# A graph network on one core: the first convolution's bias on the features instead of on attention's output, with the order around it changed

## The chip, the core and the metric

One core of a Trainium2 chip runs the whole program. The core has TensorE (PE) for matrix products, VectorE (DVE), ScalarE (ACT) and GpSimd (POOL) for elementwise work, and SyncE (SP), which issues most of the transfers. The metric is the device time of one execution in microseconds (us), as the median of several runs.

## The reference

128 graphs of 128 nodes, 512 features per node, float32 throughout. Two layers follow each other, each with a residual and a layer norm.

```
feats = x @ W                              # 8 heads of 64
e     = leaky_relu(feats@a_self [:,None] + feats@a_neigh [None,:], 0.2)
att   = softmax(e + -1e10 * (1 - adj))
x     = layernorm(x + relu(att @ feats + b))
...
H     = (adj != 0);  Dn = 1/(H @ adj[0]);  Be = 1/H.sum(0)
conv(x, W, b) = Dn * (H @ (Be * (H.T @ (x @ W.T)))) + b
h     = layernorm(relu(conv(x, W1, b1)), gamma, beta)     # 1024 features
x     = layernorm(2 * x + conv(h, W2, b2))
```

Each row of att sums to one. So att @ (feats + b) equals att @ feats + b.

## The kernel before, in words

Two graphs, g = 0 and 1, form a pair, and 64 pairs p are worked through as a software pipeline. A pair runs through four stages, each one period after the last: stage 0 prepares the adjacency matrix, stage 1 makes the features and scores, stage 2 the softmax and attention with the first norm, stages 3 and 4 the second layer. In a steady period the engines therefore work on several pairs at once.

No scheduler decides the order. Each step is a function that is registered with a stage and a time within a nominal period of 38.6: `at(2, 28.05, add_bias, ...)` is stage 2 at 28.05. At the end all steps of all pairs are sorted by (p + stage) * 38.6 + time and emitted in that order (L1223). These numbers are only keys for sorting. [...] A table `first` (L1159) and two small ones in the last loop override the keys of the first and last pairs.

Each of the three large products of a pair (features `pf`, hidden layer `ph`, second weights `py`) is done by seven half-size products instead of eight (function `chain`, L325). The products go in the order 1, 2, 6, 5, 7, 4, 3 and use three accumulators X, Y, W. Product 1 starts X; 6, 7 and 4 add to it. After 1, 6 and 7 ACT copies X away (`copy`, L343), since DVE needs those intermediate states; product 6 must wait for the first copy, 7 for the second, 4 for the third. The sums that go in are made on POOL: `x_sums` (xS, L468), `z_sums` (zS, L837) and `h_sums` (hS, L468).

Steps that matter below, by engine, with the names that the profile shows:

- DVE: `attended_pair` (L733, L734) divides attention's output by its row sums, giving y. `residual` (L748) is relu and adding of x, `moments` (L756, L757) the mean and variance. `sum_blocks` (L947 to L952) reduces the sums of squares of the hidden layer, which go through memory (`write_sums` L957, `read_sums` L963) and come back in `sum_rest` (so, L971). `y_sum` (L932) puts the second product together, `x_transpose` (L384) turns x for the next features, `edges` (L420 to L427) and `scale_edges` (hB, L434) and `nodes` (L359 to L368) prepare the adjacency matrix, `r_evict` (R, L450) makes the propagator. `largest` (nm, L610) takes row maxima. `h_sum` (L863) puts the hidden layer together. `y_scale` (L1004) normalizes, `skip` (L802) starts the output o, `o_sum` (L1021) adds to it, `e_transpose` (eT, L639) turns the exponentials.
- POOL: `add_bias` (L739) adds b to y; `rstds` (rsa and rso, L764) is the power -0.5 of a variance; `mask` (neg, L377) makes the mask and `masked` (L588) adds it to the scores nb, in four parts (g, q), q being the half of the heads; `h_means` (m, L992) and `h_rstd` (veh L997, rsh L1000) give the hidden layer's norm; `squares` (sq, L901) are folded sums.
- ACT: `leaky` (L604) and `exponential` (L618) on nb, four instructions for each part; `first_output` (L791) writes the first layer's result; `z_evict` (L826) copies the product pz out; `relu` (L878) and `square` (L889) work on the hidden layer h.
- PE: in the order of a period pz, pd, then ph with pq in it, pf with one py in it, attention pav, and the rest of py (all but attention at L97).
- SP: besides others, the row sums rd out and broadcast back as nb (L551, L569), the exponentials out (ed, L622) and back (eb, L630), sd and sums_out, and the loads of x, xb, a, w, ab.

In a steady period before the change, add_bias stands on POOL after the squares and ahead of h_means, mask, rsa and the four masked adds; on DVE sum_blocks, x_transpose 1 and residual 0 follow attended_pair, then y_sum(0,0), residual 1, the variance and y_sum(1,1). h_sum(1,1) comes after skip, hB and nodes. On ACT leaky(0,1) stands after the two z_evict.

The features `ft` hold, for each graph and head, 67 numbers: the two scores, the 64 features and a column of ones that gives attention's row sums. There are two such buffers, used by even and odd pairs.

Of the kernel before, what the change touches and what calls it, by code (L numbers as in the profile page):

```python
# [10 lines left out]
ALU = mybir.AluOpType  # L11
# [9 lines left out]
def kernel(  # L21
# [45 lines left out]
    nc = tc.nc  # L67
# [3 lines left out]
    H = 8  # L71
# [17 lines left out]
    def bank(name):  # L89
        return psum.tile([P, HALF], F32, tag="bank", name=name)  # L90
# [57 lines left out]
    UW = U + 2  # L148
# [16 lines left out]
    def everywhere(t, ap, queue):  # L165
# [5 lines left out]
    b0_bc, b2_bc, bw_bc = (  # L171
        const.tile([P, F], F32, name=n) for n in ("b0_bc", "b2_bc", "bw_bc")
    )
# [37 lines left out]
    for i in range(2):  # L211
        t = const.tile([P, 2, H, UW + 1], F32, name=f"ft{i}")
# [99 lines left out]
    LAST = PAIRS - 1  # L312
    steps = []

    def step(lag, time, since=0, until=PAIRS):

        def keep(fn):
            steps.append((lag, time, fn.__name__, range(since, until), fn, ()))
            return fn
        return keep  # L320

    def at(lag, time, fn, *args, since=0, until=PAIRS):
        steps.append((lag, time, fn.__name__, range(since, until), fn, args))

    def chain(kind, lag, times, multiply, w, extra=0, since=0, until=PAIRS):  # L325

        tag = "chain" if w == HALF else "half"

        def product(p, s, i):
            where, start = {1: ("X", 1), 2: ("Y", 1), 6: ("X", 0), 5: ("W", 1), 7: ("X", 0),
                            4: ("X", 0), 3: ("W", 0)}[i]
            if start:
                s[kind, where] = bank(f"{kind}{where}_{p}")
            multiply(s, i, s[kind, where], start)

        def copy(p, s, i):  # L340
            n = w + (extra if i < 2 else 0)
            t = s[kind, i] = work.tile([P, HALF if w == HALF else FW], F32, tag=f"{tag}_{i}", name=f"{kind}{i}_{p}")
            nc.scalar.copy(t[:, :n], s[kind, "X"][:, :n])  # L343

        for i, t in zip((1, 2, 6, 5, 7, 4, 3), times):
            at(lag, t, product, i, since=since, until=until)
        for i, t in enumerate(times[7:]):
            at(lag, t, copy, i, since=since, until=until)
# [22 lines left out]
    def write_nodes(p, s):  # L371
        s["dd"] = dram.tile([NB, B, B], F32, tag="dd", name=f"dd_d_{p}")
        nc.sync.dma_start(s["dd"].rearrange("b c n -> (b c) n"), s["dr"])
    @step(0, 30.63)
    def mask(p, s):
        s["neg"] = work.tile([P, 2, N], F32, tag="neg", name=f"neg_{p}", bufs=2)
        nc.gpsimd.tensor_scalar(s["neg"], s["a"], -1.0, BIG, op0=ALU.add, op1=ALU.mult)  # L377
# [9 lines left out]
        )  # L387

    at(0, 26.15, x_transpose, 0, since=2)
    at(0, 28.95, x_transpose, 1, since=2)  # L390

    def x_transpose_first(p, s):
        s["px"] = [bank(f"px_{p}_{g}") for g in range(2)]
# [98 lines left out]
    def feature(s, i, to, start):  # L492
# [4 lines left out]
          feature, FW, since=2)  # L497
# [155 lines left out]
        )  # L653

    for (g, q), tm, (lag, tl), (lagx, tx), te, tt in (
        ((0, 0), 31.0, (1, 33.2), (1, 36.1), 4.05, 16.6), ((0, 1), 32.2, (1, 40.63), (1, 40.68), 4.6, 16.65),
        ((1, 0), 34.2, (2, 2.05), (2, 2.1), 7.8, 21.5), ((1, 1), 35.4, (2, 6.0), (2, 7.3), 7.9, 21.55),
    ):
        at(1, tm, masked, g, q)
        at(lag, tl, leaky, g, q)  # L660
        at(lagx, tx, largest, g, q)
        at(2, te, exponential, g, q)
        at(2, tt, e_transpose, g, q, since=1)
# [72 lines left out]
            )  # L736

    def add_bias(p, s, g):
        nc.gpsimd.tensor_tensor(s["y"][:, g, :], s["y"][:, g, :], b0_bc, op=ALU.add)  # L739

    for g, t in enumerate((24.1, 29.2)):
        at(2, t, add_bias, g, until=1)
        at(2, 28.05 + 0.05 * g, add_bias, g, since=1, until=LAST)
        at(2, t, add_bias, g, since=LAST)

    def residual(p, s, g):
        y = s["y"][:, g, :]
# [22 lines left out]
        )  # L770

    at(2, 26.2, residual, 0, until=1)
    at(2, 29.0, residual, 0, since=1, until=LAST)
    at(2, 26.2, residual, 0, since=LAST)
    at(2, 30.7, residual, 1)
    at(2, 30.8, rstds, "a")

    @step(2, 33.12)
    def first_shift(p, s):
# [62 lines left out]
    def hidden(s, i, to, start):  # L842
# [4 lines left out]
        for m in range(KH // 2):  # L847
# [3 lines left out]
                    bool(start) and m == 0 and k == 0, k == KF // 2 - 1,  # L851
                )

    chain("ph", 3, (2.0, 3.8, 5.6, 7.35, 9.1, 12.65, 14.4, 4.0, 5.95, 11.0), hidden,
          HALF)

    def hid(s, g, q):
# [7 lines left out]
        )  # L865

    at(3, 5.9, h_sum, 0, 0, 0, "Y")
    at(3, 11.8, h_sum, 1, 1, 2, "W")
    at(3, 16.4, h_sum, 1, 0, 1, "W")

    def relu(p, s, g, q):
# [45 lines left out]
    def weigh(s, i, to, start):  # L917
# [3 lines left out]
          QU, 1, until=LAST)  # L921
# [62 lines left out]
            s["ve"], s["pm"][:, :2 * N].rearrange("p (g f) -> p g f", g=2), AX.X, ALU.add  # L984
        )

    @step(3, 30.62, until=LAST)
    def h_means(p, s):

        s["m2"] = small.tile([P, 2], F32, tag="m2", name=f"m2_{p}")  # L990
        for g, m in enumerate((s["y2"][:, 0, 0, QU:], s["py", 1][:, QU:QU + 1])):
            nc.gpsimd.tensor_tensor(s["m2"][:, g:g + 1], m, m, op=ALU.mult)  # L992
# [127 lines left out]
    for t, fn, *args in (  # L1120
# [40 lines left out]
        ("nodes", 0): 12.9, ("write_nodes", 0): 12.92, ("spread_nodes", 0): 15.9,  # L1161
        ("edges", 0): 14.46, ("edges", 2): 119.2,
        ("x_transpose", 2, 0): 120.5, ("x_transpose", 2, 1): 121.1, ("scale_edges", 0): 14.47, ("propagator", 0): 14.55,
        ("r_evict", 0): 99.76,
        ("spread_rows", 1): 15.72, ("nodes", 1): 15.55, ("write_nodes", 1): 15.85,
        ("edges", 1): 110.4, ("scale_edges", 1): 110.5, ("neighbours", 1): 80.1,
        ("propagator", 1): 117.76, ("spread_nodes", 1): 80.3, ("r_evict", 1): 121.8,
        ("leaky", 0, 1, 1): 77.65, ("leaky", 0, 0, 1): 73.6, ("largest", 0, 0, 1): 75.3,
        ("attend", 0, 0, 0): 78.95, ("attend", 0, 0, 1): 78.96, ("attend", 0, 1, 0): 78.97,
        ("attend", 0, 1, 1): 78.98, ("attended", 0, 0): 97.8, ("attended", 0, 1): 97.81,  # L1170
        ("add_bias", 0, 0): 97.82, ("add_bias", 0, 1): 97.83,
        ("residual", 0, 0): 99.6, ("residual", 0, 1): 99.65, ("rstds", 0, "a"): 99.7,
        ("leaky", 1, 0, 0): 117.85, ("leaky", 1, 0, 1): 117.9, ("leaky", 1, 1, 0): 119.9,
        ("largest", 1, 0, 0): 118.0, ("largest", 1, 0, 1): 118.2, ("largest", 1, 1, 0): 120.2,
        ("masked", 1, 0, 0): 109.0, ("masked", 1, 1, 1): 121.5,
# [18 lines left out]
    for p in range(PAIRS):  # L1194
        if p > 1:
            todo.append(({2: 79.5, 3: 143.1}.get(p, p * T), load, (p,)))
            todo.append((16.2 if p == 2 else p * T + 19.0, load_blocks, (p,)))
            todo.append((p * T + (28.5 if p == 2 else 20.5), load_edges, (p,)))
        for lag, time, name, pairs, fn, args in steps:
            if p not in pairs:  # L1200
                continue
            if p == 0 and lag == 2 and time < 8.5:
                time *= 0.2
            if p == LAST:

                time = {
                    ("attend", 0): 24.25, ("attended", 0): 25.5, ("add_bias", 0): 25.6,
                    ("attend", 1): 25.95, ("attended", 1): 26.0, ("add_bias", 1): 26.1,
                    ("residual", 1): 26.3, ("rstds", "a"): 26.4,
                }.get((name,) + args[:1], time)  # L1210
            if p == LAST - 1:
                time = {
                    ("product", 2): 24.22 if (lag, time) > (3, 20.0) else time,
                    ("product", 5): 29.5 if (lag, time) > (3, 20.0) else time,
                    ("squares", 0): 26.5, ("squares", 1): 26.6, ("h_sums", 2): 22.3,
                    ("h_rstd",): 4.6, ("y_scale", 1): 5.8, ("y_scale", 0): 5.9,
                }.get((name,) + args[:1], time)
            time += (p + lag) * T
            todo.append((
                first.get((name, p) + args, first.get((name, p), time)), run, (fn, p, args)  # L1220
            ))
# [46 lines left out]
```

## Time and profile before

| what | value |
|---|---|
| median of 3 runs | 2437.37 us (2436.82 to 2437.77) |
| the profiled execution, its own time | 2435.63 us |
| its span, first to last instruction | 2433.8 us |
| granted TensorE clock | 0.996 |
| PE, busy | 2390.8 us |
| DVE, busy | 1942.0 us |
| POOL, busy | 1796.8 us |
| ACT, busy | 1510.2 us |

A line of a timeline gives the start and the duration in us, engine, line of the code, operation, what it writes and reads, the shape and the count if equal instructions follow each other; in brackets how long the engine stood idle before it and what ended that. Durations of instructions that follow each other overlap a little, so distances are best taken from start to start. TensorE's ends are modelled, and its busy share alone doesn't tell a stall. The lines quoted in the prediction are from the first page and from timelines of about one period, 1536 to 1584, and of the beginning and the end.

### The profile page before, as it was taken

Reading aid. Unit: us, or ns where it says so; the run is one execution under the profiler, and the core shown is the slowest. Engines: PE = TensorE matmul, PEld = TensorE weight load, DVE = VectorE, ACT = ScalarE, POOL = GpSimd, SP = SyncE. Lnnn points to the kernel's source line nnn. Section 1 sums busy time; section 2 is a strip of 40 time slices with the busy share of each in tenths; the row PEclk is TensorE's granted clock in tenths of the full one; section 3 lists DMA queues with packets and bytes.
Section 4 is the critical chain, followed back from the end, with each engine's and each line's share of the span. In section 5 each row is a group of like instructions: output and inputs, shape, how many; then the busy total and the mean of one; then the engine's idle time right before and its main releaser. Section 6 shows DMA issues by size and latency. Waiting matters only on the chain.

```text
span 2433.8 us, 80910 instructions
## 1 busy us (share of the span) xinstructions
PE 2390.8 (98%) x32309; PEld 1989.8 (82%) x32309; DVE 1942.0 (80%) x4456; ACT 1510.2 (62%) x4481; POOL 1796.8 (74%) x2060
## 2 busy tenths in 40 slices
PE   7999999999999999999999999999999999999998
PEld 5788888888888888888888888888888888888886
DVE  7888878778878888887787788888887887888875
ACT  4665765756756656657567566576575575665663
POOL 5777777777777777777777777777777777777764
PEclk9999999999999999999999999999999999999999
DMA  6545545545455555454454555554544545555531
GB/s 186 140 141 153 146 132 152 149 133 157 140 144 148 144 146 147 137 154 140 133 153 139 147 147 145 149 148 133 154 148 133 151 145 141 147 147 146 147 119 45
DMA packets 432872, 347.10 MB, mean 143 GB/s; under 512 B 153176, under 2 KB 382064, under 8 KB 432496
## 3 DMA queue, kind: packets, MB, share of 16 engines
q1 hardware_dynamic: 429024, 337.46, 48.4%
q8 instruction: 255, 4.18, 0.7%
q10 hardware_dynamic: 3472, 4.47, 0.6%
q14 instruction: 121, 0.99, 0.1%
HBM read 239.08 MB, written 102.73 MB: 140 GB/s over the span
## 4 chain that ended last, share of the span: by engine, by line
POOL 42%; DVE 30%; PE 11%; DMA 10%; issue 4%; ACT 2%; SPq 1%; POOLq 0%; DVEq 0%; ACTq 0%
POOL nb L588 11%; POOL hS L468 9%; POOL sq L901 9%; POOL zS L837 6%; DVE y L1004 5%; DVE o L802 4%; DMA sd<-sr 3%; DMA nb<-rd 3%; DVE statso L756 3%; DVE o L1021 3%; PE pfX L97 2%; PE phX L97 2%; DVE xT L384 2%; DVE nm L610 2%; POOL rsa L764 2%
## 5 line engine op out<-in xcount | busy, mean ns | idle before, releaser
L343 ACT COPY py<-pyX 128x257 f32<-128x257 f32 x189 | 70.6, 374 | 513.0 <-PE pyX L97 513.0
L97 PEld LDWEIGHTS phX<-zS,w_sb 128*64 128x64 f32 x6144 | 345.2, 137 | 39.3 <-issue 26.3
L97 PE MATMUL phX<-zS,w_sb 128*64 128x128 f32 x6144 | 368.5, 273 | 3.1 <-POOL xS L468 2.6
L901 POOL TENSOR_TENSOR sq<-sq 128x512 f32<-128x512 f32 (+2 forms) x384 | 324.0, 844 | 20.1
L588 POOL TENSOR_TENSOR nb<-nb,neg 128x512 f32<-128x512 f32 x256 | 319.2, 1279 | 7.8 <-DMA nb<-rd 7.8
L604 ACT ACTIVATE nb<-nb,ft 128x128 f32<-128x128 f32 x1020 | 318.6, 393 | 7.2 <-POOL nb L588 7.2
L764 POOL TENSOR_TENSOR rso<-veo,mhalf 128x2 f32<-128x2 f32 x63 | 44.1, 700 | 371.9 <-DVE veo L762 371.9
L618 ACT ACTIVATE nb<-nb,nm 128x128 f32<-128x128 f32 x1024 | 314.0, 394 | 2.3 <-DVE nm L610 2.0
L878 ACT ACTIVATE h<-h,vecs 128x128 f32<-128x128 f32 x768 | 245.1, 392 | 57.3 <-DVE h L863 57.3
L610 DVE TENSOR_REDUCE nm<-nb 128x4 f32<-128x512 f32 x256 | 171.7, 682 | 127.8 <-ACT nb L604 118.0
L97 PE MATMUL pyW<-w_sb,hS 128*64 128x256 f32 x2016 | 244.3, 381 | 3.1 <-DVE y L932 3.1
L97 PE MATMUL pyX<-w_sb,hS 128*64 128x257 f32 x2016 | 245.0, 381 | 0.0
L97 PE MATMUL pyX<-w_sb,h 128*64 128x257 f32 x2016 | 243.6, 379 | 0.5 <-ACT py L343 0.5
L97 PEld LDWEIGHTS pyW<-w_sb,hS 128*64 128x64 f32 x2016 | 165.7, 136 | 62.7 <-issue 20.8
L97 PEld LDWEIGHTS pyX<-w_sb,h 128*64 128x64 f32 x2016 | 172.6, 136 | 47.3 <-ACT py L343 0.9
L97 PEld LDWEIGHTS pyX<-w_sb,hS 128*64 128x64 f32 x2016 | 167.2, 137 | 40.2
L1004 DVE SCALAR_TENSOR_TENSOR y<-y,rsh,bw_bc 128x512 f32<-128x512 f32 x126 | 147.4, 1208 | 35.1 <-POOL rsh L1000 34.8
L639 DVE STREAM_TRANSPOSE eT<-eb 128x512 f32<-128x512 f32 x252 | 163.7, 688 | 9.2 <-DMA eb<-ed 9.0
L889 ACT ACTIVATE sq<-h 128x512 f32<-128x512 f32 x256 | 160.7, 629 | 2.1
L739 POOL TENSOR_TENSOR y<-y,b_bc 128x512 f32<-128x512 f32 x128 | 160.4, 1274 | 2.1 <-DVE rden L733 1.5
L468 POOL TENSOR_TENSOR hS<-h 128x512 f32<-128x512 f32 x126 | 159.1, 1282 | 1.7 <-ACT h L878 1.7
L508 DVE TENSOR_TENSOR ft<-pf,pfW 128x264 f32<-128x264 f32 x124 | 53.2, 429 | 125.9 <-PE pfW L97 80.9
(178 smaller groups left out, 5616.1 us busy)
## 6 DMA issues: line engine op xcount, KB each, us to landing
nb<-rd SPq DMA_DIRECT2D x127, 512.0 KB
ed<-nb SPq DMA_DIRECT2D x126, 512.0 KB
eb<-ed SPq DMA_DIRECT2D x504, 128.0 KB
x<-in_x_dram SPq DMA_DIRECT2D x64, 512.0 KB
out_dram<-o SPq DMA_DIRECT2D x63, 512.0 KB
xb<-in_x_dram SPq DMA_DIRECT2D x248, 128.0 KB
a<-in_adj_dram SPq DMA_DIRECT2D x64, 128.0 KB
w<-in_adj_dram SPq DMA_DIRECT2D x128, 64.0 KB
```

The costliest lines, as they stand in the source:

```text
L97: nc.tensor.matmul(to[rows], lhs[:, rows], rhs, start=start, stop=stop, skip_group_check=True)
L468: engine.tensor_tensor(t[:, i], in0, in1, op=op)
L588: nc.gpsimd.tensor_tensor(t, t, neg[:, :, None, :].to_broadcast([P, NB, HH, B]), op=ALU.add)
L604: nc.scalar.activation(t, t, AF.Prelu, bias=s["ft"][:, g, h, 0:1], alpha=SLOPE)
L610: nc.vector.tensor_reduce(s["nm"][:, g, hs], scores(p, s, g, hs).rearrange("p b h j -> p h b j"), AX.XY, ALU.max, negate=True,)
L618: nc.scalar.activation(t, t, AF.Exp, bias=s["nm"][:, g, h:h + 1])
L639: nc.vector.transpose(s["eT"][:, g, hs, :].rearrange("p h (b i) -> p h b i", b=NB), s["eb", g][:, :, hs, :].rearrange("p b h j -> p h b j"),)
L739: nc.gpsimd.tensor_tensor(s["y"][:, g, :], s["y"][:, g, :], b0_bc, op=ALU.add)
L878: nc.scalar.activation(dst[:, k, :], src[:, k, :], AF.Relu, bias=b1_sb[:, c:c + 1])
L889: nc.scalar.activation(s["sq"][:, g, q * KH // 2:(q + 1) * KH // 2, :], hid(s, g, q), AF.Square, scale=DH ** -0.5,)
L901: nc.gpsimd.tensor_tensor(t[:, :n, :], t[:, :n, :], t[:, n:2 * n, :], op=ALU.add)
L1004: nc.vector.scalar_tensor_tensor(t, t, s["rs", "h"][:, g:g + 1], bw_bc.rearrange("p (j c) -> p j c", j=2), op0=ALU.mult, op1=ALU.add,)
```

## The change

The bias is added to the 64 features of every head in ft, in place, and no longer to y. It is one POOL instruction per graph as before. Its key is stage 2 at 9.0, which puts it after x_sums and ahead of rso on POOL, and after the last leaky, which reads the two score columns of the same buffer. For the first pair it comes before the masks.

In steady periods the order then is:

- DVE: attended_pair, residual 0, residual 1, variance, sum_blocks, y_sum(0,0), y_sum(1,1), x_transpose 1, edges, nm(0,0), y_sum(0,1), nm(0,1), R. Further on h_sum(1,1) stands after skip and ahead of hB and nodes.
- POOL: squares, mask, rsa, four masked adds, h_means, then z_sums, veh and rsh, x_sums, two bias adds, rso.
- ACT: leaky(0,0), the copy of py into y (L930), leaky(0,1), two z_evict, leaky(1,0), exponential(0,0), the first copy of phX, exponential(0,1).
- SP: the order of its transfers is the same.
- PE: the order is the same.

```diff
-    @step(0, 30.63)
+    @step(0, 28.25)
     def mask(p, s):
...
-    at(0, 28.95, x_transpose, 1, since=2)
+    at(0, 35.0, x_transpose, 1, since=2)
...
-        ((0, 0), 31.0, (1, 33.2), (1, 36.1), 4.05, 16.6), ((0, 1), 32.2, (1, 40.63), (1, 40.68), 4.6, 16.65),
+        ((0, 0), 31.0, (1, 33.2), (1, 36.1), 3.9, 16.6), ((0, 1), 32.2, (1, 37.3), (1, 38.75), 4.6, 16.65),
...
     def add_bias(p, s, g):
-        nc.gpsimd.tensor_tensor(s["y"][:, g, :], s["y"][:, g, :], b0_bc, op=ALU.add)
-
-    for g, t in enumerate((24.1, 29.2)):
-        at(2, t, add_bias, g, until=1)
-        at(2, 28.05 + 0.05 * g, add_bias, g, since=1, until=LAST)
-        at(2, t, add_bias, g, since=LAST)
+
+        t = s["ft"][:, g, :, 2:UW]
+        nc.gpsimd.tensor_tensor(
+            t, t, b0_bc.rearrange("p (h u) -> p h u", h=H), op=ALU.add
+        )
+
+    for g in range(2):
+        at(2, 9.0 + 0.05 * g, add_bias, g)
...
-    at(2, 29.0, residual, 0, since=1, until=LAST)
+    at(2, 28.1, residual, 0, since=1, until=LAST)
     at(2, 26.2, residual, 0, since=LAST)
-    at(2, 30.7, residual, 1)
-    at(2, 30.8, rstds, "a")
+    at(2, 28.2, residual, 1)
+    at(2, 28.3, rstds, "a")
...
-    chain("ph", 3, (2.0, 3.8, 5.6, 7.35, 9.1, 12.65, 14.4, 4.0, 5.95, 11.0), hidden,
+    chain("ph", 3, (2.0, 3.8, 5.6, 7.35, 9.1, 12.65, 14.4, 4.0, 5.95, 10.7), hidden,
...
-    at(3, 11.8, h_sum, 1, 1, 2, "W")
+    at(3, 10.75, h_sum, 1, 1, 2, "W")
...
-    @step(3, 30.62, until=LAST)
+    @step(3, 36.0, until=LAST)
     def h_means(p, s):
...
-        ("r_evict", 0): 99.76,
+        ("r_evict", 0): 97.845,
...
-        ("attend", 0, 1, 1): 78.98, ("attended", 0, 0): 97.8, ("attended", 0, 1): 97.81,
-        ("add_bias", 0, 0): 97.82, ("add_bias", 0, 1): 97.83,
-        ("residual", 0, 0): 99.6, ("residual", 0, 1): 99.65, ("rstds", 0, "a"): 99.7,
+        ("attend", 0, 1, 1): 78.98, ("attended", 0, 0): 97.8, ("attended", 0, 1): 97.82,
+        ("add_bias", 0, 0): 13.6, ("add_bias", 0, 1): 13.61,
+        ("residual", 0, 0): 97.81, ("residual", 0, 1): 97.83, ("rstds", 0, "a"): 97.84,
...
-                    ("attend", 0): 24.25, ("attended", 0): 25.5, ("add_bias", 0): 25.6,
-                    ("attend", 1): 25.95, ("attended", 1): 26.0, ("add_bias", 1): 26.1,
+                    ("attend", 0): 24.25, ("attended", 0): 25.5,
+                    ("attend", 1): 25.95, ("attended", 1): 26.0,
```

## The prediction

> **What bounds the kernel now.** First the page: TensorE is busy for all but 43 us of the span, and no other engine is above 80%.
>
> ```profile
> PE 2390.8 (98%) x32309; PEld 1989.8 (82%) x32309; DVE 1942.0 (80%) x4456; ACT 1510.2 (62%) x4481; POOL 1796.8 (74%) x2060
> ```
>
> Second, TensorE's timeline. Product pz of one pair starts at 1542.99 and, 21 pairs on, at 2322.20: 37.11 us a pair. (From 130.47 it is 59 pairs at 37.15; one irregular pair near 1208 costs 1.7.) Below, T is the time after the pz at 1542.99.
>
> ```profile
> 1544.73 0.64 PE L97 MATMUL pd<-hT,hB 128*64 128x128 f32 x8
> 1545.42 1.97 PE L97 MATMUL phX<-zT,w_sb 128*64 128x128 f32 x32
> ...
> 1560.31 1.06 PE L97 MATMUL pfY<-w_sb,xT 128*64 128x264 f32 x8
> 1561.48 1.11 PE L97 MATMUL pfX<-w_sb,xS 128*64 128x264 f32 x8
> 1562.39 1.09 PE L97 MATMUL pfW<-w_sb,xS 128*64 128x264 f32 x8
> 1563.28 1.09 PE L97 MATMUL pfX<-w_sb,xS 128*64 128x264 f32 x8
> ```
>
> Read start to start, since ends overlap. pd to phX is 0.69, pfY to pfX is 1.17; near the end of the same trace, where other engines have less to do, the same two take 0.44 (2360.66 to 2361.10) and 0.89 (2339.57 to 2340.46). So TensorE stalls 0.25 and 0.28 there. Another 0.05 follows in phX (1.80 for 1.75), 0.02 in pfX, and 0.11 at the last pyX and pyW (1.83 and 1.76 for 1.73). All stalls: 0.71 us a pair, the most a pair can gain.
>
> Third, who ends them. ACT's timeline: phX waits for z_evict (L826), queued behind leaky (L604); pfX waits for the copy of pfX (L343), queued behind relu and squares that came late because h_sum(1,1) (L863) did.
>
> ```profile
> 1560.98 0.36 ACT L343 COPY pf<-pfX 128x264 f32<-128x264 f32 x1
> 1561.23 1.28 ACT L878 ACTIVATE h<-h,vecs 128x128 f32<-128x128 f32 x4
> 1562.63 0.38 ACT L343 COPY pf<-pfX 128x264 f32<-128x264 f32 x1
> ```
>
> The second copy (T 19.64) gates the pfX at T 20.29, and stands in ACT's queue behind relu(1,0), which needs DVE's h_sum(1,0) at 1560.48. Nothing waits there now, but the slack is only 0.2.
>
> Fourth, DVE and POOL in that stretch.
>
> ```profile
> 1550.65 2.35 DVE L1004 SCALAR_TENSOR_TENSOR y<-y,rsh,bw_bc 128x512 f32<-128x512 f32 x2 [0.39 <-POOL rsh L1000]
> 1552.93 0.67 DVE L610 TENSOR_REDUCE nm<-nb 128x4 f32<-128x512 f32 x1
> 1553.52 1.81 DVE L802 SCALAR_TENSOR_TENSOR o<-y,b_bc 128x512 f32<-128x512 f32 x2
> 1555.26 0.47 DVE L434 TENSOR_SCALAR hB<-hT,deg 128x128 f32<-128x128 f32 x2
> ...
> 1556.91 0.65 DVE L863 TENSOR_TENSOR h<-ph,phW 128x512 f32<-128x512 f32 x1
> ...
> 1560.48 0.68 DVE L863 TENSOR_TENSOR h<-ph,phW 128x512 f32<-128x512 f32 x1
> ```
>
> ```profile
> 1553.56 1.23 POOL L468 TENSOR_TENSOR xS<-xT,xS 128x256 f32<-128x256 f32 x1
> 1560.65 0.70 POOL L764 TENSOR_TENSOR rso<-veo,mhalf 128x2 f32<-128x2 f32 x1 [5.87 <-DVE veo L762]
> ```
>
> DVE has no gap from y_scale to h_sum(1,0), 9.8 us. POOL has one of 5.87, and the moved bias lands at its head.
>
> [...] the two y_scale take 2.35 beside POOL's xS and 1.42 without POOL (2366.15); skip 1.81 and 1.28 (2368.97); xS 1.23 and 0.73 (1550.59). [...] in the first pair:
>
> ```profile
> 51.52 2.28 DVE L434 TENSOR_SCALAR hB<-hT,deg 128x128 f32<-128x128 f32 x2
> ```
>
> Beside three masked adds on POOL (49.99 for 3.72) the two hB take 2.28 instead of 0.47, and end with POOL. [...] I take the old bias's 1.27 (L739)[...].
>
> **The change part by part.**
> Bias. Two POOL adds of 1.27 leave the stretch from attention to the masks, two enter after xS (L468). Nothing waits for their result before attention, 12 us later; the cost is who they block.
>
> Residual path. attended ends at 1571.74. Both residuals now follow at once: 2 x 1.55 + 0.2 of DVE, so rsa (L764) starts about 1575.2 instead of 1577.91, and h_means and its wait for y_sum no longer stand ahead. masked can then start when nb has landed. One piece of the chain of waits shows that landing at 1242.40, and the next pz starts at 1245.49: T -3.1. The adds thus end near T 1.8 instead of 3.5. leaky(0,1), now ahead of z_evict, ends near T 0.9, when z_evict(0) cannot yet start: the 0.25 and 0.05 go. If the landing is 1 us later, half of that stays.
>
> The mask (0.40) goes ahead of rsa into time in which POOL is idle: nothing. sum_blocks comes 3.3 later on DVE, so write_sums and, behind it on SP, the load of x do too. SP is otherwise idle from 1575.05 to 1581.09, until sd lands behind nb; rd, the same size, needs 2.0 where little is ahead of it, so an issue near T -3.6 still lands by T 1. I take nothing; 1 us is the upper end. x_transpose 1 has a whole period. y_sum(1,1) now runs before x_transpose, with 1 us to spare: 0.11 goes.
>
> z_sums and on. h_means (0.8) now stands between masked and z_sums, to T 2.6; z_evict(1) ends about T 2.54, so zS starts T 2.67 instead of 3.46. rsh, xS and y_scale shift by 0.79.
>
> Now the new collision. I play the lock through, each instruction taking turns: xS4 T 9.8 to 10.5 ([...] nm waits for leaky(1,1) until T 9.48). skip 1 waits for it: to 11.1. bias 0 waits for skip 1: to 12.2. skip 2 waits for bias 0: to 12.8 (alone, DVE would be through at 11.4). bias 1: to 13.9. h_sum(1,1), moved ahead of hB, takes T 12.7 to 13.3: 1.2 earlier than now, so the copy at pfX is in time and its 0.28 + 0.02 go. hB waits for bias 1: done 14.2. Then nodes, o_sum and moments as now: before, from the end of hB (12.67) to h_sum(1,0) (17.49) less the moved h_sum (0.57) is 4.27. h_sum(1,0) starts at T 18.5, 1.0 later than now. Queued behind the waiting hB are all of these; who waits for them is ACT's relu(1,0) and, behind that in ACT's queue, the copy of pfX.
>
> From there: 0.72 to relu, 1.20 for four, 0.38 copy, 0.12 to TensorE: pfX at T 20.9. Without stalls TensorE would be there at 19.67; now it is at 20.29. A new stall of 1.2 takes the place of 0.62, plus 0.6; the 0.11 comes off. Net +0.49 a pair; 60 pairs: +29.
>
> Late transfers (nb, sums_out) put zS and both bias adds up to 1 us later in some pairs: +6. First pair: TensorE idles 7.52 before its first pz (50.81), at the end of a chain attended, bias, residual, rsa, first_output, in which two bias adds (2.49) and four updates of w_sb (L299, 1.66) lie; the adds go to POOL's wait for nb (7.38 idle before 28.51), the updates behind R. That is 4.2 at most; pd then waits for hB, so 2.3 at least; I take 3.5. In the last pair 1.96 of waiting for eT (2381.61) shrink as exponentials come earlier: 1.5, from 0 to 2. Sum: 29 + 6 - 5 = +30 on the profiled execution (span 2433.8, its own time 2435.63), 2465.6; the runs' median, 2437.37, is 1.7 above that execution: 2467.
>
> **Rivals.**
> A. The bias hides in POOL's gap. h_sum(1,0) comes by T 17.25 and all stalls go: 0.70 x 60 = 42, and 5: 2390. For it: the gap, and that 36.72 occurs as a period here (2322.20 to 2358.92). Against it: both lock readings. It decides below T 17.98 for h_sum(1,0), where the stall gained equals that lost.
> B. The turns fall otherwise (one skip gets in ahead, or only hB waits): h_sum(1,0) near T 18, and the kernel is where it was: 2437, less the ends.
> C. sd or a longer bias: 0.5 to 0.7 more on the same chain: 2500.
>
> **How the numbers follow.** Forecast 0.61, A 0.24, B 0.09, C 0.06. Within 0.2% (4.9 us) is about what this measurement can't tell from no change: most of B, and a little of the forecast's lower end. Faster 0.25, same 0.08, slower 0.67. The likeliest case's own range is 2445 to 2490; the range reaches down through B to a half gain and up to C: 2420 to 2500, leaving most of A and little else.
>
> **What would show it.** Right: pd to phX 0.44 and pfY to pfX 0.89, but pfW to pfX near 2 instead of 0.89; skip over 2 and hB over 0.8 a couple; h_sum(1,0) near T 18.5; rsa near T -4.7; the irregular pair gone. Wrong: hB at 0.47, skip at 1.3, h_sum(1,0) by T 17.3. Also wrong: z_evict late behind leaky(0,1), so that pd's stall stays, or DVE's so (L971) waiting longer than now for sums_out.

## The result and the profile after

The changed kernel takes 2444.25 us (median, 2442.99 to 2446.81). Against runs of the kernel before on the same chip the ratio is 1.003, 95% interval 1.0012 to 1.0047: slower, by some 7 us where 30 were forecast. The profiled execution took 2442.99, its span is 2440.8 (before: 2433.8).

First the page: the busy times, and three groups. In a group's line the last part is the idle time of the engine just before the group's instructions, in us over the whole span, and what ended it.

```profile
PE 2369.9 (97%) x32309; PEld 2009.1 (82%) x32309; DVE 2000.1 (82%) x4456; ACT 1524.7 (62%) x4481; POOL 1816.2 (74%) x2060
...
L588 POOL TENSOR_TENSOR nb<-nb,neg 128x512 f32<-128x512 f32 x256 | 319.6, 1281 | 37.6 <-DMA nb<-rd 37.1
...
L880 ACT ACTIVATE h<-h,vecs 128x128 f32<-128x128 f32 x768 | 239.5, 393 | 76.7 <-DVE h L865 76.4
...
L741 POOL TENSOR_TENSOR ft<-ft,b_bc 128x512 f32<-128x512 f32 x128 | 203.9, 1613 | 6.4 <-ACT ft L532 6.4
```

DVE is busy 58 us longer with the same 4456 instructions: skip is busy 162.1 us in all for 115.8 before, hB 55.1 for 32.5. The bias adds show 1.61 each instead of 1.27. ACT's relu (L880) waits 76 us in all for DVE's h_sum, before 57. (Lines behind the bias have moved by two: L863 is now L865, L802 is L804, L878 is L880.)

TensorE's timeline, a pair whose pz starts at 1550.69. As in the prediction, T is the time after a pz.

```profile
1552.44 0.63 PE L97 MATMUL pd<-hT,hB 128*64 128x128 f32 x8
1552.87 1.94 PE L97 MATMUL phX<-zT,w_sb 128*64 128x128 f32 x32
...
1567.71 1.09 PE L97 MATMUL pfY<-w_sb,xT 128*64 128x264 f32 x8
1568.60 1.09 PE L97 MATMUL pfX<-w_sb,xS 128*64 128x264 f32 x8
1569.49 1.09 PE L97 MATMUL pfW<-w_sb,xS 128*64 128x264 f32 x8
1571.22 1.11 PE L97 MATMUL pfX<-w_sb,xS 128*64 128x264 f32 x8 [0.64 <-ACT pf L343]
```

Start to start: pd to phX is 0.43 (before 0.69), pfY to pfX 0.89 (1.17). But pfW to pfX is 1.73, before 0.89: a stall of 0.84. The 0.64 in the brackets is less than 0.84, since the modelled ends of matmuls overlap; distances of starts are the measure.

What ends that stall: the chain of waits of the same stretch, start and duration.

```profile
1568.82 0.69 DVE h L865
1569.51 0.02 issue
1569.53 0.20 ACT h L880
...
1569.84 0.97 ACT h L880 x3
1570.81 0.27 ACT pf L343
1571.08 0.14 issue
1571.22 1.11 PE pfX L97 x8
```

It is the path of the prediction: h_sum(1,0) on DVE, four relu, the copy of pfX, TensorE. And why h_sum(1,0) is late, on DVE and on POOL:

```profile
1560.14 0.69 DVE L610 TENSOR_REDUCE nm<-nb 128x4 f32<-128x512 f32 x1 [0.24 <-ACT nb L604]
1560.74 2.59 DVE L804 SCALAR_TENSOR_TENSOR o<-y,b_bc 128x512 f32<-128x512 f32 x2
1563.25 0.68 DVE L865 TENSOR_TENSOR h<-ph,phW 128x512 f32<-128x512 f32 x1
1563.85 0.81 DVE L434 TENSOR_SCALAR hB<-hT,deg 128x128 f32<-128x128 f32 x2
...
1568.82 0.68 DVE L865 TENSOR_TENSOR h<-ph,phW 128x512 f32<-128x512 f32 x1
```

```profile
1560.45 0.73 POOL L468 TENSOR_TENSOR xS<-xT,xS 128x256 f32<-128x256 f32 x1
1561.15 3.23 POOL L741 TENSOR_TENSOR ft<-ft,b_bc 128x512 f32<-128x512 f32 x2
1568.99 0.70 POOL L766 TENSOR_TENSOR rso<-veo,mhalf 128x2 f32<-128x2 f32 x1 [4.61 <-DVE veo L764]
```

The two skips take 2.59 for 1.81 before, the two hB 0.81 for 0.47; h_sum(1,0), behind them on DVE, starts at T 18.13 (before 17.51, both medians over the steady pairs). Over 53 steady pairs of each of the two traces every period has the same order of instructions, 69 on DVE, 32 on POOL and 70 on ACT; skip and hB stand ahead of h_sum(1,0) in all of them. The typical period, the median of the steady ones, is 37.23 instead of 37.11.

Where the 7.0 of span come from: at the third pz the changed kernel is 2.2 behind (132.67 for 130.47); over the 59 steady pairs to the pz at 2332.92 it falls back by another 8.5, some 7 of them in the typical pairs (59 x 0.12); the last two periods win back 3.7.

### The profile page after: what moved, and what is told of

It reads as the page before. It is cut to its first block, busy times and chain, and to the rows that moved or that the text cites. A ratio compares the mean times of both kernels' runs of the same rounds, so it can differ in the third digit from the quotient of the medians.

```text
span 2440.8 us, 81033 instructions
## 1 busy us (share of the span) xinstructions
PE 2369.9 (97%) x32309; PEld 2009.1 (82%) x32309; DVE 2000.1 (82%) x4456; ACT 1524.7 (62%) x4481; POOL 1816.2 (74%) x2060
## 4 chain that ended last, share of the span: by engine, by line
PE 83%; DVE 6%; ACT 5%; DMA 2%; issue 2%; POOL 1%; SPq 0%; ACTq 0%; POOLq 0%; DVEq 0%
PE pyX L97 17%; PE phX L97 16%; PE pyW L97 8%; PE phW L97 7%; PE pfX L97 7%; PE phY L97 4%; PE pav L702 4%; PE pz L97 4%; PE pyY L97 4%; PE pq L97 4%; ACT h L880 3%; PE pfW L97 2%; DVE h L865 2%; PE pfY L97 2%; PE pd L97 1%
## 5 line engine op out<-in xcount | busy, mean ns | idle before, releaser
L97 PEld LDWEIGHTS phX<-zS,w_sb 128*64 128x64 f32 x6144 | 350.3, 137 | 38.1 <-POOL ft L741 23.1
L903 POOL TENSOR_TENSOR sq<-sq 128x512 f32<-128x512 f32 (+2 forms) x384 | 349.6, 911 | 20.1
L588 POOL TENSOR_TENSOR nb<-nb,neg 128x512 f32<-128x512 f32 x256 | 319.6, 1281 | 37.6 <-DMA nb<-rd 37.1
L604 ACT ACTIVATE nb<-nb,ft 128x128 f32<-128x128 f32 x1020 | 325.3, 392 | 19.2 <-POOL nb L588 17.3
L618 ACT ACTIVATE nb<-nb,nm 128x128 f32<-128x128 f32 x1024 | 319.1, 391 | 4.0 <-DVE nm L610 4.0
L880 ACT ACTIVATE h<-h,vecs 128x128 f32<-128x128 f32 x768 | 239.5, 393 | 76.7 <-DVE h L865 76.4
L97 PEld LDWEIGHTS pyW<-w_sb,hS 128*64 128x64 f32 x2016 | 171.5, 136 | 47.2 <-POOL neg L377 0.8
L741 POOL TENSOR_TENSOR ft<-ft,b_bc 128x512 f32<-128x512 f32 x128 | 203.9, 1613 | 6.4 <-ACT ft L532 6.4
L97 PE MATMUL pfX<-w_sb,xS 128*64 128x264 f32 x992 | 136.2, 390 | 40.3 <-ACT pf L343 40.1
L804 DVE SCALAR_TENSOR_TENSOR o<-y,b_bc 128x512 f32<-128x512 f32 x128 | 162.1, 1305 | 0.0
```

The lines of the kernel that those rows point to most:

```text
L97: nc.tensor.matmul(to[rows], lhs[:, rows], rhs, start=start, stop=stop, skip_group_check=True)
L588: nc.gpsimd.tensor_tensor(t, t, neg[:, :, None, :].to_broadcast([P, NB, HH, B]), op=ALU.add)
L604: nc.scalar.activation(t, t, AF.Prelu, bias=s["ft"][:, g, h, 0:1], alpha=SLOPE)
L618: nc.scalar.activation(t, t, AF.Exp, bias=s["nm"][:, g, h:h + 1])
L741: nc.gpsimd.tensor_tensor(t, t, b0_bc.rearrange("p (h u) -> p h u", h=H), op=ALU.add)
L804: nc.vector.scalar_tensor_tensor(s["o"][:, g, :], s["y"][:, g, :], 2.0, b2_bc, op0=ALU.mult, op1=ALU.add)
```

## The experiments

My theory: the bias adds on POOL and skip and hB on DVE shut each other out (this is the lock; the readings for it so far are durations, 2.59 for 1.81 and 0.81 for 0.47), h_sum(1,0) behind them comes late, and TensorE waits for the copy behind relu. Rivals: the reordering itself makes h_sum(1,0) late; the lock hurts elsewhere; transfers bind. Ratios are against the kernel before on the same chip.

**No bias.**

```diff
-        at(2, 9.0 + 0.05 * g, add_bias, g)
+        at(2, 9.0 + 0.05 * g, add_bias, g, until=1)
```

> The changed kernel without its bias adds in all pairs but the first (the first convolution's bias is left out there); all else, order included, is as changed. Theory (the two POOL adds lock out skip and hB on DVE, which makes h_sum(1,0) late): skip falls from 2.6 to about 1.4 a couple, hB from 0.8 to 0.47, h_sum(1,0) starts near T 16.6 instead of 18.1, the wait of TensorE for the copy of pfX (0.84 a pair) is gone, the period falls from 37.23 to about 36.4, the time to about 2395. Rival (the reordering itself, h_sum(1,1) and h_means in new places, makes h_sum(1,0) late): skip and hB get shorter, but the period stays near 37.2 and the time near 2440.

Measured: 2415.16 us, ratio 0.9907 (0.9893 to 0.992). The bias costs the changed kernel some 30 us (1.003 less 0.9907 of 2437); the rest of the change, with no add left anywhere in these pairs, gains 23. DVE, pair with pz at 974.21:

```profile
984.27 1.58 DVE L804 SCALAR_TENSOR_TENSOR o<-y,b_bc 128x512 f32<-128x512 f32 x2
986.48 0.69 DVE L865 TENSOR_TENSOR h<-ph,phW 128x512 f32<-128x512 f32 x1 [0.62 <-ACT ph L343]
987.08 0.48 DVE L434 TENSOR_SCALAR hB<-hT,deg 128x128 f32<-128x128 f32 x2
...
991.72 0.68 DVE L865 TENSOR_TENSOR h<-ph,phW 128x512 f32<-128x512 f32 x1
```

Without the adds the skips take 1.58 for 2.59 and the hB 0.48 for 0.81, so the lock is shown. But h_sum(1,0) starts at T 17.52, not 16.6: DVE now stands idle for 0.62 ahead of h_sum(1,1), until ACT's third copy of phX, and hB follows only at 987.08, behind h_sum(1,1). That idle time is cover that I had not seen: the lock makes the skips 0.9 longer, of which only 0.29 reach h_sum(1,1). With 0.32 at hB the bias costs 0.61 at h_sum(1,0), and TensorE's stall there is 0.23 instead of 0.84. Nor does the time fall to 2395: 0.23 stays, and in 21 of 57 pairs (after the change: 6) the period is over 0.2 above the typical 36.62. POOL's wait for the transfer of nb (L588) doubles, from 37.1 to 73.5 us in all.

**The bias alone, in the old order.** Only add_bias as in the change, with its keys; residual, mask, leaky and h_sum(1,1) as before.

> The kernel before with only the bias moved: the adds are made on ft behind x_sums, as in the change, and everything else keeps its old place. Theory (lock): the adds hold up skip and hB by about 1.3 to 1.6, so h_sum(1,1), which still stands behind hB, and h_sum(1,0) start that much later (near T 18.7 for the latter); the period rises from 37.11 to 37.7 to 38.2, the time to 2475 to 2500. Rival (the adds are harmless in POOL's gap, and what the change lost comes from its reordering): the period stays at 37.1 or falls, the time is 2437 or less.

Measured: 2533.11 us, ratio 1.0391 (1.0377 to 1.0405), typical period 38.77. The rival falls; the effect is far larger than I expected. TensorE and DVE, pair with pz at 1026.17:

```profile
1042.56 1.97 PE L97 MATMUL phW<-zT,w_sb 128*64 128x128 f32 x32 [1.66 <-DVE h L865]
```

```profile
1036.59 1.81 DVE L804 SCALAR_TENSOR_TENSOR o<-y,b_bc 128x512 f32<-128x512 f32 x2
1038.32 2.35 DVE L434 TENSOR_SCALAR hB<-hT,deg 128x128 f32<-128x128 f32 x2
...
1041.86 0.65 DVE L865 TENSOR_TENSOR h<-ph,phW 128x512 f32<-128x512 f32 x1
```

hB, 0.4 to 0.5 before, takes 2.35 and is through at 1040.67; the two bias adds beside it on POOL, 2.77 from 1037.82, are through at 1040.59. h_sum(1,1), behind it, reads accumulator W, and the last ph product may not add to W before that: a wait of 1.85 (start to start 3.60 for 1.75) that I had not on my list.

**The bias and h_sum(1,1) ahead of hB.**

```diff
-    at(3, 11.8, h_sum, 1, 1, 2, "W")
+    at(3, 10.75, h_sum, 1, 1, 2, "W")
```

(with the copy's key 11.0 made 10.7, both on the kernel with the bias alone)

> The kernel before with the moved bias, as measured at 2533, and one more part of the change: h_sum(1,1) ahead of hB. Theory (that run was so slow because the last ph product has to wait until h_sum(1,1), stuck behind the locked hB, has read accumulator W): the wait of 1.85 there goes; what stays is h_sum(1,0) near T 18.7 and a wait of about 1.1 at the fifth pf product. Period 37.8 to 38.2, time 2475 to 2500. Rival (h_sum(1,1) is not what was late, other parts of the reordering make up for it): time 2525 or more.

Measured: 2493.38 us, ratio 1.0231 (1.0214 to 1.0247); period 38.16, h_sum(1,0) at T 18.81, the stall at the fifth pf product 1.2. As expected. Step by step, each against the kernel before: the bias alone costs 95 us, with h_sum(1,1) ahead of hB 56, with the rest of the reordering, the whole change, 7.

**One add of two.**

```diff
-        at(2, 9.0 + 0.05 * g, add_bias, g)
+        at(2, 9.0 + 0.05 * g, add_bias, g, until=(PAIRS, 1)[g])
```

> The changed kernel with the bias added for the first graph of each pair only (the second graph's is left out, but in the first pair). Theory (the two adds each take one turn from DVE: the first from the second skip, the second from the first hB): skip stays at 2.6 a couple, hB falls from 0.8 to 0.47, h_sum(1,0) starts near T 17.8, the wait at the fifth pf product is about 0.5, the time 2425 to 2435. Rivals: the skip alone decides (h_sum(1,0) stays at 18.1, 2444), or the hB alone (as without any bias, T 17.5, 2415).

Measured: 2426.68 us, ratio 0.9957 (0.9941 to 0.9973); h_sum(1,0) at T 17.79, stall 0.50. DVE, pz at 981.31:

```profile
991.37 2.58 DVE L804 SCALAR_TENSOR_TENSOR o<-y,b_bc 128x512 f32<-128x512 f32 x2
...
994.47 0.47 DVE L434 TENSOR_SCALAR hB<-hT,deg 128x128 f32<-128x128 f32 x2
```

As expected: the first add holds up the second skip, the second add holds up hB, and each costs h_sum(1,0) about 0.3 (T 17.52 with no add, 17.79 with one, 18.13 with two). Both rivals fall.

**The bias later.** In the changed kernel, key 9.0 made 15.7: behind rso.

> The changed kernel with the two bias adds behind rso on POOL instead of behind x_sums; nothing else moved. Theory (lock at skip and hB): as without the bias, skip 1.6 and hB 0.47 a couple, h_sum(1,0) near T 17.5, the wait of TensorE at the fifth pf product 0.2 instead of 0.84; against it the squares and h_sums come 2.5 later on POOL, which costs 0 to 0.6. Period 36.6 to 37.1, time 2412 to 2440. Rival (the place doesn't matter, POOL's extra work as such does): period 37.2 or more, time 2444 or more.

Measured: 2483.99 us, ratio 1.0193 (1.0179 to 1.0208): a miss. The first half came as expected (skip 1.56, hB 0.47, h_sum(1,0) at T 17.48, stall 0.19). The other end was mis-sized; TensorE and POOL, pz at 1007.35:

```profile
1034.83 1.96 PE L97 MATMUL pyX<-w_sb,hS 128*64 128x257 f32 x16 [1.11 <-POOL hS L468]
```

```profile
1025.67 2.53 POOL L741 TENSOR_TENSOR ft<-ft,b_bc 128x512 f32<-128x512 f32 x2
...
1033.52 1.26 POOL L468 TENSOR_TENSOR hS<-hS,h 128x512 f32<-128x512 f32 x1
```

This pyX needs the third h_sums, not, as I took it, the second; all of them come 2.5 later than without the bias, and 1.3 a pair is lost. The time alone would fit the rival (POOL's work as such, 2444 or more). The trace does not fit it: the same two adds cost a stall at pfX in one place and at pyX in the other, by what stands behind them.

**h_sum(1,0) first.** What costs is that h_sum(1,0) stands last on DVE, so I moved it. A first try, with key 14.0, stood ahead of the product that it reads:

> The changed kernel with one step moved on DVE: h_sum(1,0) stands ahead of the two moments and the variance of o, no longer behind them. The bias and its collision stay. Theory (what costs is only that h_sum(1,0) is late for relu and, behind it, the copy of pfX): h_sum(1,0) near T 16.4, no wait at the fifth pf product, period 36.4, time about 2395, with skip and hB as long as in the changed kernel. Rival (the lock hurts somewhere else as well, or rso, the squares and the h_sums behind it on POOL come too late by the 0.6): the period stays over 36.8, the time over 2415.

It took 2652.94 us; it sums W before the last product has been added, so it leaves that product out of the hidden layer, and says nothing on the theory. With the key behind the product:

```diff
-    at(3, 16.4, h_sum, 1, 0, 1, "W")
+    at(3, 14.6, h_sum, 1, 0, 1, "W")
```

> The changed kernel with one step moved on DVE: h_sum(1,0) right behind the product that it reads, and so ahead of the two moments and the variance of o. The bias and its collision stay. Theory (the collision costs only because h_sum(1,0) comes late for relu and the copy behind it): h_sum(1,0) near T 16.4 instead of 18.1, skip and hB as long as in the changed kernel, no wait at the fifth pf product, typical period near 36.4, time 2398 to 2412, faster than both kernels. Rival (the lock hurts elsewhere too, or rso, the squares and h_sums on POOL come too late by the 0.6): period over 36.9, time over 2425.

Measured: 2423.66 us, ratio 0.9945 (0.9931 to 0.9959), faster than both kernels. h_sum(1,0) starts at T 16.34, pfW to pfX is 0.89 again, while skip (2.58) and hB (0.81) are as long as in the changed kernel: the lock no longer reaches the copy of pfX. But the time misses the expected 2398 to 2412, and the typical period is 36.71, not 36.4; part of the rival holds. The moments of o, and with them rso, squares and h_sums on POOL, come 0.6 later, and TensorE loses 0.33 before the same pyX.

**Squares ahead of rso.** To bring the h_sums forward:

```diff
-            at(3, ((17.0, 17.1, 17.2), (26.0, 27.3, 28.0))[g][level], squares, g, level)
+            at(3, ((15.92, 15.94, 15.96), (26.0, 27.3, 28.0))[g][level], squares, g, level)
...
-    at(4, 15.6, rstds, "o", until=LAST)
+    at(4, 16.0, rstds, "o", until=LAST)
```

> The kernel with h_sum(1,0) ahead of the moments of o, in which TensorE's new wait of 0.28 was for the h_sums, and one more move: on POOL the squares of the first graph go ahead of rso (rso and its variance only behind them), so that the squares run while POOL would wait for the variance, and the h_sums start about 2 earlier. Theory (that wait came from rso, later by 0.6, holding up squares and h_sums): the wait before pyX from h_sums is gone, typical period 36.4, time 2402 to 2414, faster than both kernels. Rival (the bound is by now the transfers of nb, late in many pairs, so that a shorter period only makes more pairs late): typical period 36.4 in few pairs, the mean not below 36.85, time 2420 or more.

> The same order as the kernel with the squares ahead of rso, but without the bias adds in all pairs but the first (the bias is left out there). Theory (with h_sum(1,0) out of the locked chain, the two adds cost nothing any more): the time is within 5 us of that kernel with its bias. Rival (the lock still costs something on another path): faster than it by more than 10 us.

Measured: 2462.54 us, ratio 1.009 (1.0077 to 1.0104), and without the bias 2457.83, 1.0076 (1.0062 to 1.0089). The first expectation fell, its theory and its rival: the typical period is 37.28. DVE and TensorE:

```profile
1575.54 2.89 DVE L769 TENSOR_SCALAR o<-o,mvo,rso 128x512 f32<-128x512 f32 x2
```

```profile
1579.26 1.11 PE L97 MATMUL pfW<-w_sb,xS 128*64 128x264 f32 x8 [0.49 <-DVE ft L508]
```

The wait for h_sums is gone, but they now meet the two o_norm (L769), which take 2.89 instead of 1.45. Behind them on DVE stand the sums that free the accumulator for pfW (start to start 1.57 for 0.89) and the transposes for attention. The same lock, elsewhere. The second expectation held, with 4.7 us of 2460 for the two adds. But it proves less than I wanted: rso, behind the squares, starts at T 19.43 with the bias and 19.41 without, so in this order the squares cover what the lock delays, and the stall at o_norm bounds both kernels. The next run is the better test.

**Only the last fold moved.** From the kernel with h_sum(1,0) first, so that the short folds stay beside o_norm:

```diff
-            at(3, ((17.0, 17.1, 17.2), (26.0, 27.3, 28.0))[g][level], squares, g, level)
+            at(3, ((17.0, 17.1, 22.3), (26.0, 27.3, 28.0))[g][level], squares, g, level)
```

> The kernel with h_sum(1,0) ahead of the moments of o (2424, typical period 36.71, TensorE waiting 0.33 before the pyX that needs the third h_sums), and on POOL the last fold of the first graph's squares, 0.5 long, moved behind the third h_sums; the two longer folds stay beside o_norm. Theory (the 0.33 is only that POOL's queue is 0.6 late there): the third h_sums ends 0.5 earlier, that wait is gone, typical period 36.4, time 2405 to 2416. Rival (the h_sums, now earlier, take turns from o_norm on DVE, as they did where all the squares stood ahead of rso, or the transfers of nb bound the pairs): time 2424 or more.

Measured: 2408.84 us, ratio 0.9875 (0.9859 to 0.9892), the fastest of all. TensorE, pz at 974.78:

```profile
993.57 1.07 PE L97 MATMUL pfW<-w_sb,xS 128*64 128x264 f32 x8
994.46 1.07 PE L97 MATMUL pfX<-w_sb,xS 128*64 128x264 f32 x8
...
998.87 2.04 PE L702 MATMUL pav<-ft,eT 128*64 128x65 f32 x64
1000.74 1.92 PE L97 MATMUL pyX<-w_sb,hS 128*64 128x257 f32 x16
```

Every distance is that of an unstalled product (0.89 from pfW to pfX, 1.87 from pav to pyX), and the typical period is 36.37, with the bias adds where the change put them. And the lock is still there, on DVE in the same pair:

```profile
984.81 2.57 DVE L804 SCALAR_TENSOR_TENSOR o<-y,b_bc 128x512 f32<-128x512 f32 x2
...
987.90 0.81 DVE L434 TENSOR_SCALAR hB<-hT,deg 128x128 f32<-128x128 f32 x2
...
991.12 0.69 DVE L865 TENSOR_TENSOR h<-ph,phW 128x512 f32<-128x512 f32 x1
```

So in a typical pair the locked skip and hB cost TensorE nothing, once nothing behind them is urgent. The mean is 36.70, for late pairs, 19 of 57. In such pairs nb's transfer is issued near T -8 instead of -9.8 and lands up to 3 later; that this is the next bound is argued from the trace, not tried.

**The first pairs.**

```diff
+        ("exponential", 1, 0, 0): 2 * T + 42.65, ("leaky", 2, 0, 1): 3 * T + 40.63, ("largest", 2, 0, 1): 3 * T + 40.68,
```

> The changed kernel with three keys of the first pairs set back: exponential(0,0) of the second pair behind the first copy of phX, leaky(0,1) and its maximum of the third pair behind the two z_evict. Theory (the changed kernel lost its 2.7 at the first pz again because ACT's queue has these ahead of what TensorE waits for): the third product of ph in the first period no longer waits 1.8, pd to phX in the second shrinks from 1.99 to below 1; the third pz comes 2 to 3 earlier, the time is 2441 to 2442. Rival (POOL or DVE, late through the bias adds in the first period, are as late): the third pz stays where it is, near 132.7, and the time at 2444.

Measured: 2449.16 us, ratio 1.0051 (1.0037 to 1.0065); the interval overlaps that of the change, so the time decides nothing. The trace does decide. In the changed kernel TensorE's first two periods have these waits among others:

```profile
59.21 1.97 PE L97 MATMUL phX<-zS,w_sb 128*64 128x128 f32 x32 [1.79 <-ACT ph L343]
...
66.83 1.97 PE L97 MATMUL phX<-zS,w_sb 128*64 128x128 f32 x32 [2.16 <-POOL xS L468]
...
97.22 1.97 PE L97 MATMUL phX<-zT,w_sb 128*64 128x128 f32 x32 [1.38 <-ACT zT L828]
```

With the keys set back the first is 0.65, but the second 3.26; the third 0.21, but 0.98 of waiting stands ahead of the second pz. The third pz comes 1.1 earlier (131.56), less than the 2 to 3 expected, and even that is not the keys' doing: in this execution the first pz, which stands ahead of every moved key, already comes 1.4 earlier (46.74 for 48.13). From the first pz to the third it takes 84.8, in the changed kernel 84.5. The waits named shrink, and others take their place: the theory falls, these were not what bound the two periods.

## Why the prediction was right and wrong

Right were the sign, the bound and the path. The stalls that were to go went: pd to phX 0.44, pfY to pfX 0.89, the last py products 1.73; rsa starts at T -4.87 (said: near -4.7), zS at 2.64 (2.67), and skip is over 2, hB over 0.8. DVE waits less for sums_out than before (57.7 us in all for 81.8). One sign came only in part: the irregular pair near 1208 is gone, but four pairs between 207 and 358 are now 0.2 to 1.0 longer. The new stall came at the product named, through the chain named. That the instructions take turns one by one was an estimate, made from longer durations such as y_scale's 2.35 for 1.42; the trace shows strict turns: xS to T 10.49, skip to 11.04, bias to 12.09, skip to 12.64, bias to 13.69, hB behind it to 13.97. The nm ahead of them takes none: in the pair above it runs for 0.38 beside xS, and neither is longer than elsewhere (0.69 and 0.73).

Wrong was one size. The step that failed is "h_sum(1,0) starts at T 18.5", with its "new stall of 1.2":

| step | forecast, T or us | measured |
|---|---|---|
| first skip done | 11.1 | 11.04 |
| first bias done | 12.2 | 12.09 |
| second skip done | 12.8 | 12.64 |
| second bias done | 13.9 | 13.69 |
| hB done | 14.2 | 13.97 |
| from there to h_sum(1,0) | 4.27 | 4.16 |
| h_sum(1,0) starts | 18.5 | 18.13 |
| new stall | 1.2 | 0.84 |
| net a pair | +0.49 | +0.12 |
| steady pairs | +29 | +7 |
| late transfers | +6 | +1.5 |
| first pairs | -3.5 | +2.2 |
| last pairs | -1.5 | -3.7 |
| sum | +30 | +7.0 |

No turn is out by more than 0.06. But all five were taken too long, 0.23 together; 0.11 more came from the way from hB to h_sum(1,0), read off one pair: its 12.67 is the start of the instruction behind hB, while hB's line ends at T 12.74, and 17.49 less 12.67 less 0.57 is 4.25, not 4.27 (the medians are 4.20 before and 4.16 after). Rounding the sum added 0.03. That made 0.37. The net is the small difference of two larger stalls, 1.2 less 0.71, and is counted 60 times, so 0.37 is 22 of the 23 us by which the sum is off; what was wrong in the late transfers, the start and the end nearly cancels, by luck. A working that ends in such a difference should have carried this error into the range of its likeliest case, which began at 2445, just above the result.

Rival A, where the bias hides, was not within reach: without any bias h_sum(1,0) would be at 17.52, above the 17.25 that it needed. Rival B named the right place, T 18, for another reason: the turns fell as played.

Late transfers were mis-sized, too: only 6 pairs in 57 are visibly longer, against 3 before. For the first pair I saw what the first pz would gain (it came 2.7 earlier, 48.13 for 50.81; in the other kernels that start like the changed one it comes at 46.47 to 48.09, so over 1 us of this differs between executions) and did not ask what is late next. In the two kernels that take only the rows of add_bias from the new table `first`, the first pz is 2.1 to 2.5 earlier and the second at 92.35 and 91.64, for 92.37: most of the gain doesn't last one period. In the changed kernel the first period is 3.7 longer than before. The exponential ahead of the copy of phX isn't the cause, as the last experiment shows. The updates (L299), moved behind R on DVE, are my guess. No run tried it, but the traces speak for it. DVE in the changed kernel:

```profile
45.97 0.42 DVE L450 TENSOR_TENSOR R<-pd,dnb 128x256 f32<-128x256 f32 x1
46.30 1.65 DVE L299 SCALAR_TENSOR_TENSOR w_sb<-w_sb,vecs,gw 128x256 f32<-128x256 f32 x4
47.87 1.65 DVE L299 SCALAR_TENSOR_TENSOR w<-w,vecs,gw 128x256 f32<-128x256 f32 x4
...
64.22 0.73 DVE L610 TENSOR_REDUCE nm<-nb 128x4 f32<-128x512 f32 x1
```

Before, the same R starts at 50.22, with both groups ahead of it, and the same nm at 64.01; DVE has no gap between the two in either kernel. So by the time of this nm R's 4.2 us are spent, 3.1 of them on the two groups. ACT's exponential waits for it, and behind that the third copy of phX, so the phX at 66.83 starts 0.2 later than before (66.62); its bracket names POOL's xS, but the copy ends later, at 66.73 for 66.43. In the two kernels with only the rows of add_bias, where both groups stay ahead of R, it starts at 64.68 and 64.15. At the end the wait for eT (1.96) went, as said, and with it 1.3 at the next pyX that I had left out: it took 3.06 from start to start, now 1.74.

## What to carry to other kernels

When instructions of two engines lengthen each other, as the bias adds did with skip (2.59 beside them, 1.58 without) and hB (0.81 and 0.48), ask first what stands behind the lengthened one in its queue: here the same two adds cost 95 us in the old order, 56 with one step moved ahead of the lengthened hB, 30 in the changed order, and no stall in a typical pair of the last order. Of the 0.9 by which the skips grew here, only 0.29 reached the step behind them, since 0.62 of idle time would have followed them anyway, so look for such cover before adding up turns. And when a forecast is the difference of two stalls times a count of pairs, take the durations as medians over many pairs, carry the error of each step through the count, and widen the range by it.

## What the runs showed of the hardware that was not expected

- What the lock delays shows as duration, on both engines: a bias add shows 1.64 in the changed kernel, but its turn above takes 1.05, and in the first period, beside one h_sum and two hB on DVE, two adds take 2.33, while those two hB take 1.44 instead of 0.47. That the add on strips of 64 features out of 67 takes the old bias's 1.27 was an estimate of the forecast; there it took no longer, 1.17 each.
- Which POOL work met a DVE instruction mattered as much as how long it was: beside squares that get shorter (1.28, 0.80, 0.52) two o_norm take 1.45 in the kernels before and after and 1.94 with h_sum(1,0) first, beside two h_sums, 2.68 together, they take 2.89.
- How long POOL waited for a transfer changed with the rest, and not simply with the period: it waits 7.8 us in all for nb in the kernel before (typical period 37.11), 37.1 in the changed one (37.23), 73.5 in that without bias (36.62), 85.1 with the squares first (37.28) and 47.5 in the fastest (36.37), though the transfer is the same 512 KB each time.
